# A two-layer graph kernel: the features of pair 2 moved ahead of pair 0's propagation, pair 1's exponentials transposed on TensorE, column sums of the weights in four column tiles

## The chip, the cores and the metric

The kernel runs on one core of a Trainium2 chip. The metric is device time in microseconds of one execution, without a profiler; it is given as the median of several runs. Engines are named as the profile names them: PE is TensorE (matmul), DVE is VectorE, ACT is ScalarE, POOL is GpSimd, SP is SyncE, which here only issues DMAs.

## The reference, cut to what matters

For each of 128 graphs with 128 nodes of 512 features, a graph attention layer and then a hypergraph convolution, each with a residual and a layer norm:

```python
# layer 0, for each graph b and each of 8 heads h (64 features each)
feats = einsum('bnf,hfu->bhnu', X, W)
dense = leaky_relu(e_self[..., :, None] + e_neigh[..., None, :], 0.2)   # e_* = feats . a_self, a_neigh
att = softmax(dense - 1e10 * (1 - A), axis=-1)
x = layernorm(X + relu(einsum('bhij,bhju->bhiu', att, feats) + b))
# layer 1: P(v) = D^-1 H B^-1 H^T v with H = (adj != 0)
h = layer_norm(relu(P(x @ W1.T) + b1), gamma, beta)
x = layernorm(x + P(h @ W2.T) + b2)
```

Everything is float32. W is 512 x 512 over all heads, W1 is 1024 x 512, W2 is 512 x 1024.

## The kernel before, in words

**Pairs and stages.** The graphs are worked on in 64 pairs, p = 0 to 63. A pair passes through these stages. Its rows are loaded as `xb` (four DMAs of 128 KB in a blocked form, L129) and transposed on DVE to `xT` (L385, two per pair). The matrix product `pf` gives the features `ft` with the two scores of each head beside them. The scores of the neighbours go through DRAM (`rd`, L552) and come back broadcast to all partitions as `nb` (two DMAs of 512 KB, L570). POOL adds the mask (`masked`, L589), ACT the node's own score with the leaky slope (L605), DVE takes the row maximum `nm` (L611), and ACT exponentiates in place (L619), so that `nb` then holds the exponentials. These are transposed to `eT`. For pairs from 1 on this is done through DRAM: written in one piece per graph as `ed` (L623), read back in blocks as `eb` (L631), and transposed block by block on DVE (L640). For pair 0 PE transposes them (`e_transpose_first`, `pet`, L651) and copies bring them out of PSUM (L652). `pav` (L703) multiplies `eT` by `ft`; `attended` (L714, L734 and L735), `residual` (L751 to L760) and `rstds` (`vea`, L765) lead to the normalized `y` (ACT, L794).

**Layer 1.** `edges` (L421 to L428) makes H^T and its degrees from the adjacency `ab` (L137), `scale_edges` (`hB`, L435) scales them, and `propagator` and `r_evict` (`pd`, `R`, L451) give P as a matrix. `pz` multiplies y by `R`; `zT` is copied out (L829). The chain `ph` multiplies by W1, `h_sum` and `relu` (L866, L881) give `h`, and the chain `py` multiplies by W2. `skip` (L805) makes `o` from `y` and b2, to which the output is added later.

**Products in seven parts.** `pf`, `ph` and `py` are each done by `chain` as seven products of halves in place of eight, in the order 1, 2, 6, 5, 7, 4, 3, into three PSUM banks X, Y and W; between them ACT copies X out (L344). They need sums of quarter blocks: of the rows (`xS`, `zS`, `hS`, made by POOL) and of the weights (made once at the start; `second_sums`, L226, for W2, by `prepare_output_block_sums`; L249 for W1). Product 4 of `py` uses the last of W2's sums, which is called `t4` below. `columns` (L97) issues each matmul as two tiles of 64 columns.

**Weights at the start.** gamma, beta and the mean over h are folded into W2. For this `prepare_output` multiplies W2 by the two columns `gbs` (`pv`, L276), `prepare_output_spread` spreads the result over all partitions (`gw`, `bw`, L288), and `prepare_output_blocks` rewrites the blocks of W2 (L300). Pairs 0 and 1 use plain products for `pf` and transposes of x and adjacency on PE.

**Order.** Each engine works through its instructions in the order in which the program issues them. That order is written by hand: every step has a pair lag and a time, `at(lag, time, fn, ...)`; its place is (p + lag) * 38.6 + time, the dictionary `first` puts other values in place of it for the first pairs, and the list `todo` is sorted by it. So the numbers only sort and aren't real times. SP's queue holds all loads and stores in that order; an issue that waits for a buffer holds back everything behind it. `nb`, `xb`, `ab` and `hB` have one buffer each, `R` has three. PSUM has eight banks, which go round. When `pair 1's propagation` is spoken of, that is the `pz` at 87.06 us in the profile.

Of the kernel before, what the change touches and what calls it, by code (L numbers as in the profile page):

```python
# [8 lines left out]
F32 = mybir.dt.float32  # L9
# [11 lines left out]
def kernel(  # L21
# [45 lines left out]
    nc = tc.nc  # L67
# [180 lines left out]
        )[i]  # L248
        engine.tensor_tensor(dst, in0, in1, op=op)  # L249

    gbs = const.tile([P, KH, 2], F32, name="gbs")
    made = {}

    def prepare_vectors():
# [9 lines left out]

    def prepare_rows():

        made["sel"] = work.tile([2, 2, P], F32, tag="zT", name="sel")
        nc.gpsimd.tensor_copy(
            made["sel"], ident[:2, :2].unsqueeze(2).to_broadcast([2, 2, P])
        )  # L270

    def prepare_output():
        pv = made["pv"] = [bank(f"pv{j}") for j in range(2)]
        for blk, i, j in w2_blocks:
            for k in range(KH // 2):
                nc.tensor.matmul(  # L276
                    pv[j][:2, :QU], gbs[:, i * KH // 2 + k, :], blk[:, k, :],
                    start=(i == 0 and k == 0), stop=(i == 1 and k == KH // 2 - 1),
                )

    def prepare_output_sums():
        made["sums"] = const.tile([2, F], F32, name="sums")
        for j in range(2):
            nc.vector.tensor_copy(made["sums"][:, j * QU:(j + 1) * QU], made["pv"][j][:2, :QU])

    def prepare_output_spread(c, name):
        made[name] = bank(name)
# [38 lines left out]
    def chain(kind, lag, times, multiply, w, extra=0, since=0, until=PAIRS):  # L326

        tag = "chain" if w == HALF else "half"

        def product(p, s, i):
            where, start = {1: ("X", 1), 2: ("Y", 1), 6: ("X", 0), 5: ("W", 1), 7: ("X", 0),
                            4: ("X", 0), 3: ("W", 0)}[i]
            if start:
                s[kind, where] = bank(f"{kind}{where}_{p}")
            multiply(s, i, s[kind, where], start)

        def copy(p, s, i):
            n = w + (extra if i < 2 else 0)
            t = s[kind, i] = work.tile([P, HALF if w == HALF else FW], F32, tag=f"{tag}_{i}", name=f"{kind}{i}_{p}")
            nc.scalar.copy(t[:, :n], s[kind, "X"][:, :n])  # L344

        for i, t in zip((1, 2, 6, 5, 7, 4, 3), times):
# [190 lines left out]
    @step(1, 25.0)  # L537
    def spread_rows(p, s):


        rows = work.tile([P, B], F32, tag="rows", name=f"rows_{p}")
        nc.vector.transpose(
            rows.rearrange("p (c x) -> p c x", c=2),
            s["ft"][:, :, :, :2].rearrange("p g h c -> p c (g h)"),
        )
        shape = [B, NB, B] if p == 0 else [NB, B, B]
        rd = s["rd"] = dram.tile(shape, F32, tag="rd", name=f"rd_{p}")
        if p == 0:
            for b in range(NB):
                (nc.sync, nc.scalar)[b % 2].dma_start(rd[:, b, :], rows[b * B:(b + 1) * B])  # L550
        else:
            nc.sync.dma_start(rd.rearrange("b c j -> (b c) j"), rows)  # L552

    def blocked(p, t):

        dims = "p (h b j) -> p b h j" if p == 0 else "p (b h j) -> p b h j"
        return t.rearrange(dims, b=NB, h=H)

    @step(1, 27.0)
    def neighbours(p, s):  # L560
        s["nb"] = work.tile([P, 2, H * N], F32, tag="nb", name=f"nb_{p}")
        for g in range(2):
            dst, src, hs = s["nb"][:, g, :], s["rd"], slice((2 + g) * H, (3 + g) * H)
            if p == 0:
# [5 lines left out]
            queue.dma_start(dst, src.partition_broadcast(P))  # L570
# [74 lines left out]
    def e_transpose_first(p, s, g, q):  # L645
        if (g, q) == (0, 0):
            s["eT"] = work.tile([P, 2, H, N], F32, tag="eT", name=f"eT_{p}")
        t = bank(f"pet_{g}{q}")
        for h in range(HH):
            n = (q * HH + h) * N  # L650
            nc.tensor.transpose(t[:, h * N:(h + 1) * N], s["nb"][:, g, n:n + N], ident)  # L651
# [470 lines left out]
    for t, fn, *args in (  # L1122
# [24 lines left out]
        (120.7, prepare_hidden, (nc.gpsimd, 2)), (110.6, prepare_hidden, (nc.vector, 3)),  # L1147
        (15.5, prepare_output_vectors, ()), (16.0, prepare_output, ()),
        (78.3, prepare_rows, ()), (78.79, prepare_output_sums, ()),
        (78.99, prepare_output_spread, (0, "gw")), (98.0, prepare_output_spread, (1, "bw")),  # L1150
        (98.1, prepare_output_bias, ()), (98.2, prepare_output_blocks, (slice(0, 1),)),
        (99.75, prepare_output_blocks, (slice(1, 2),)),
        (117.8, prepare_output_blocks, (slice(2, 3),)),
        (118.1, prepare_output_blocks, (slice(3, 4),)),
# [36 lines left out]
    for p, time, fn, *args in (  # L1191
# [5 lines left out]
        (1, 15.6, plain_features_out), (1, 97.9, adj_transpose_first),  # L1197
        (0, 78.8, e_transpose_first, 0, 0), (0, 78.85, e_transpose_first, 0, 1),
        (0, 78.9, e_transpose_first, 1, 0), (0, 78.93, e_transpose_first, 1, 1),
    ):  # L1200
        todo.append((time, run, (fn, p, args)))
    for p in range(PAIRS):
        if p > 1:
            todo.append(({2: 79.5, 3: 143.1}.get(p, p * T), load, (p,)))
            todo.append((16.2 if p == 2 else p * T + (19.0 if p == 3 else 2.0), load_blocks, (p,)))
            todo.append((p * T + (28.5 if p == 2 else 20.5), load_edges, (p,)))
        for lag, time, name, pairs, fn, args in steps:
            if p not in pairs:
                continue
# [66 lines left out]
```

## Time and profile before

| what | value |
|---|---|
| median of 3 runs | 2395.96 us |
| lowest and highest | 2395.58, 2396.99 us |
| the profiled execution, own time | 2395.3 us |
| its span, first to last instruction | 2393.4 us |
| granted TensorE clock, mean | 0.996 of full |
| busy: PE, DVE, ACT, POOL | 2360.8, 2089.6, 1528.5, 1825.6 us |
| PE busy in 0 to 45, 45 to 90, 90 to 135 us | 34.28, 40.26, 41.00 us |
| DVE busy in the same | 29.89, 44.17, 39.28 us |

Busy time is the sum over an engine's instructions; idle time of PE is 2393.4 less 2360.8, about 33 us, most of it in the first 160 us. The profile prints a line of kernel code as L and its number. In a timeline a line is the start in us, the duration in us, the engine, the line, the operation, its result and inputs with their shapes, and the number of instructions taken together; in brackets stands the idle time of the engine just before and the instruction that ended it.

### The profile page before, as it was taken

Reading aid. Unit: us, or ns where it says so; the run is one execution under the profiler, and the core shown is the slowest. Engines: PE = TensorE matmul, PEld = TensorE weight load, DVE = VectorE, ACT = ScalarE, POOL = GpSimd, SP = SyncE. Lnnn points to the kernel's source line nnn. Section 1 sums busy time; section 2 is a strip of 40 time slices with the busy share of each in tenths; the row PEclk is TensorE's granted clock in tenths of the full one; section 3 lists DMA queues with packets and bytes.
Section 4 is the critical chain, followed back from the end, with each engine's and each line's share of the span. In section 5 each row is a group of like instructions: output and inputs, shape, how many; then the busy total and the mean of one; then the engine's idle time right before and its main releaser. Section 6 shows DMA issues by size and latency. Waiting matters only on the chain.

```text
span 2393.4 us, 80729 instructions
## 1 busy us (share of the span) xinstructions
PE 2360.8 (99%) x32309; PEld 2026.8 (85%) x32309; DVE 2089.6 (87%) x4456; ACT 1528.5 (64%) x4481; POOL 1825.6 (76%) x2060
## 2 busy tenths in 40 slices
PE   7899999999999999999999999999999999999998
PEld 6788887888888888888888888888888888888886
DVE  7989888898898898898898888988988988988975
ACT  4565765756667667667667666666676676676662
POOL 5877786777877877877877778778778778778774
PEclk9999999999999999999999999999999999999999
DMA  6555454555554555555545555544545555555541
GB/s 197 133 148 150 143 144 134 159 143 147 151 148 144 149 148 148 151 143 154 144 142 157 141 147 155 146 146 147 150 143 153 147 150 139 148 156 140 149 128 37
DMA packets 431134, 347.09 MB, mean 145 GB/s; under 512 B 151440, under 2 KB 380328, under 8 KB 430760
## 3 DMA queue, kind: packets, MB, share of 16 engines
q1 hardware_dynamic: 427288, 337.46, 49.5%
q8 instruction: 256, 4.19, 0.7%
q10 hardware_dynamic: 3472, 4.47, 0.6%
q14 instruction: 118, 0.97, 0.2%
HBM read 239.08 MB, written 102.73 MB: 143 GB/s over the span
## 4 chain that ended last, share of the span: by engine, by line
PE 89%; DMA 4%; DVE 3%; ACT 1%; POOL 1%; issue 1%; SPq 1%; DVEq 0%; POOLq 0%; ACTq 0%
PE phX L97 17%; PE pyX L97 17%; PE pfX L97 8%; PE pyW L97 8%; PE phW L97 8%; PE pav L703 5%; PE phY L97 4%; PE pz L97 4%; PE pfW L97 4%; PE pq L97 4%; PE pyY L97 4%; PE pfY L97 2%; DMA ed<-nb 1%; PE pd L97 1%; DMA nb<-rd 1%
## 5 line engine op out<-in xcount | busy, mean ns | idle before, releaser
L344 ACT COPY py<-pyX 128x257 f32<-128x257 f32 x189 | 70.7, 374 | 538.5 <-PE pyX L97 465.6
L97 PEld LDWEIGHTS phX<-zS,w_sb 128*64 128x64 f32 x6144 | 350.6, 137 | 36.3 <-POOL ft L742 23.1
L97 PE MATMUL phX<-zS,w_sb 128*64 128x128 f32 x6144 | 373.4, 273 | 2.6 <-ACT ph L344 2.6
L904 POOL TENSOR_TENSOR sq<-sq 128x512 f32<-128x512 f32 (+2 forms) x384 | 343.9, 896 | 20.1
L589 POOL TENSOR_TENSOR nb<-nb,neg 128x512 f32<-128x512 f32 x256 | 319.9, 1284 | 23.1 <-DMA nb<-rd 12.7
L605 ACT ACTIVATE nb<-nb,ft 128x128 f32<-128x128 f32 x1020 | 325.1, 392 | 13.7 <-POOL nb L589 13.7
L619 ACT ACTIVATE nb<-nb,nm 128x128 f32<-128x128 f32 x1024 | 319.4, 392 | 4.2 <-DVE nm L611 4.0
L767 POOL TENSOR_TENSOR rso<-veo,mhalf 128x2 f32<-128x2 f32 x63 | 44.2, 701 | 338.4 <-DVE veo L765 338.4
L97 PE MATMUL pyX<-w_sb,hS 128*64 128x257 f32 x2016 | 245.1, 380 | 0.0
L97 PE MATMUL pyX<-w_sb,h 128*64 128x257 f32 x2016 | 243.7, 379 | 0.5 <-ACT py L344 0.5
L97 PE MATMUL pyW<-w_sb,hS 128*64 128x256 f32 x2016 | 243.3, 378 | 0.0
L881 ACT ACTIVATE h<-h,vecs 128x128 f32<-128x128 f32 x768 | 239.4, 394 | 2.0 <-DVE h L866 1.4
L611 DVE TENSOR_REDUCE nm<-nb 128x4 f32<-128x512 f32 x256 | 175.2, 684 | 48.8 <-ACT nb L605 46.2
L97 PEld LDWEIGHTS pyX<-w_sb,h 128*64 128x64 f32 x2016 | 173.7, 136 | 46.2 <-ACT py L344 0.9
L97 PEld LDWEIGHTS pyW<-w_sb,hS 128*64 128x64 f32 x2016 | 174.7, 136 | 43.6 <-issue 0.3
L742 POOL TENSOR_TENSOR ft<-ft,b_bc 128x512 f32<-128x512 f32 x128 | 203.9, 1613 | 6.1 <-ACT ft L533 6.1
L97 PEld LDWEIGHTS pyX<-w_sb,hS 128*64 128x64 f32 x2016 | 168.7, 137 | 38.7 <-issue 0.8
L640 DVE STREAM_TRANSPOSE eT<-eb 128x512 f32<-128x512 f32 x252 | 163.5, 685 | 5.7 <-DMA eb<-ed 4.7
L805 DVE SCALAR_TENSOR_TENSOR o<-y,b_bc 128x512 f32<-128x512 f32 x128 | 164.7, 1325 | 0.0
L1006 DVE SCALAR_TENSOR_TENSOR y<-y,rsh,bw_bc 128x512 f32<-128x512 f32 x126 | 150.1, 1229 | 14.9 <-POOL rsh L1002 14.9
L469 POOL TENSOR_TENSOR hS<-h 128x512 f32<-128x512 f32 x126 | 162.1, 1287 | 0.0
L892 ACT ACTIVATE sq<-h 128x512 f32<-128x512 f32 x256 | 160.6, 629 | 2.1
(178 smaller groups left out, 5672.4 us busy)
## 6 DMA issues: line engine op xcount, KB each, us to landing
nb<-rd SPq DMA_DIRECT2D x127, 512.0 KB, 5.6
ed<-nb SPq DMA_DIRECT2D x126, 512.0 KB, 3.4
eb<-ed SPq DMA_DIRECT2D x504, 128.0 KB, 2.9
x<-in_x_dram SPq DMA_DIRECT2D x64, 512.0 KB, 4.0
out_dram<-o SPq DMA_DIRECT2D x63, 512.0 KB, 2.9
xb<-in_x_dram SPq DMA_DIRECT2D x248, 128.0 KB, 5.5
a<-in_adj_dram SPq DMA_DIRECT2D x64, 128.0 KB, 2.4
w<-in_adj_dram SPq DMA_DIRECT2D x128, 64.0 KB, 5.0
```

Of the source, the lines that this page charges most:

```text
L97: nc.tensor.matmul(to[rows], lhs[:, rows], rhs, start=start, stop=stop, skip_group_check=True)
L469: engine.tensor_tensor(t[:, i], in0, in1, op=op)
L589: nc.gpsimd.tensor_tensor(t, t, neg[:, :, None, :].to_broadcast([P, NB, HH, B]), op=ALU.add)
L605: nc.scalar.activation(t, t, AF.Prelu, bias=s["ft"][:, g, h, 0:1], alpha=SLOPE)
L611: nc.vector.tensor_reduce(s["nm"][:, g, hs], scores(p, s, g, hs).rearrange("p b h j -> p h b j"), AX.XY, ALU.max, negate=True,)
L619: nc.scalar.activation(t, t, AF.Exp, bias=s["nm"][:, g, h:h + 1])
L640: nc.vector.transpose(s["eT"][:, g, hs, :].rearrange("p h (b i) -> p h b i", b=NB), s["eb", g][:, :, hs, :].rearrange("p b h j -> p h b j"),)
L742: nc.gpsimd.tensor_tensor(t, t, b0_bc.rearrange("p (h u) -> p h u", h=H), op=ALU.add)
L805: nc.vector.scalar_tensor_tensor(s["o"][:, g, :], s["y"][:, g, :], 2.0, b2_bc, op0=ALU.mult, op1=ALU.add)
L881: nc.scalar.activation(dst[:, k, :], src[:, k, :], AF.Relu, bias=b1_sb[:, c:c + 1])
L892: nc.scalar.activation(s["sq"][:, g, q * KH // 2:(q + 1) * KH // 2, :], hid(s, g, q), AF.Square, scale=DH ** -0.5,)
L904: nc.gpsimd.tensor_tensor(t[:, :n, :], t[:, :n, :], t[:, n:2 * n, :], op=ALU.add)
```

## The change

Three things are done, all in the first pairs.

- **Column sums.** `gbs` is padded from 2 to 32 columns, and the 32 matmuls of `pv` become 16, of which four at a time write to four column tiles of 32 in one bank; `sel` sums the four tiles while it spreads them, and the sums are copied in one piece.
- **Pair 2's features.** Pair 2's `xb` is loaded ahead of the W1 blocks. Its `xT` transposes, `xS` sums and five of its `pf` products (1, 2, 6, 5, 7) now stand before pair 0's `pz`, the other two (4, 3) right behind it.
- **Pair 1's exponentials** are transposed on PE, as those of pair 0, with all four copies out of PSUM on DVE; `ed` and `eb` begin with pair 2. `rd` of pair 1 is written in pair 0's layout, with four DMAs for one.

To fit these, the times of other steps move. On DVE, `edges(1)`, the rewriting of W2's blocks, the fourth sum of W1 and pair 0's `skip` (now two separate steps) change places; `t4`, `edges(2)` and `hB(2)` move from before pair 1's `attended` to behind its `residual`, where `edges(2)`, `hB(2)`, `R(1)`, `vea(1)` and then `t4` follow one another. On SP, the `xb` loads of pair 3 stand behind the `nb` loads of pair 2 (before: ahead of them). From pair 1's propagation on, the order on every engine is unchanged.

The core of the diff:

```diff
-    gbs = const.tile([P, KH, 2], F32, name="gbs")
+    gbs = work.tile([P, KH, B], F32, tag="y", name="gbs")
+    nc.gpsimd.memset(gbs, 0.0)
+    one = small.tile([P, 2], F32, tag="one", name="one", bufs=1)
...
     def prepare_output():
-        pv = made["pv"] = [bank(f"pv{j}") for j in range(2)]
-        for blk, i, j in w2_blocks:
-            for k in range(KH // 2):
-                nc.tensor.matmul(
-                    pv[j][:2, :QU], gbs[:, i * KH // 2 + k, :], blk[:, k, :],
-                    start=(i == 0 and k == 0), stop=(i == 1 and k == KH // 2 - 1),
-                )
+
+        t = made["pv"] = bank("pv")
+        for n in range(2):
+            for j in range(2):
+                for c in range(NB):
+                    k = 2 * c + n
+                    blk = w2_blocks[2 * (k // (KH // 2)) + j][0]
+                    nc.tensor.matmul(
+                        t[c * B:(c + 1) * B, j * QU:(j + 1) * QU], gbs[:, k, :],
+                        blk[:, k % (KH // 2), :], start=(n == 0 and j == 0), stop=(n == 1),
+                        skip_group_check=True,
+                    )
...
-        shape = [B, NB, B] if p == 0 else [NB, B, B]
+        shape = [B, NB, B] if p < 2 else [NB, B, B]
...
-        (nc.scalar.copy if q else nc.vector.tensor_copy)(
+        (nc.scalar.copy if q and p == 0 else nc.vector.tensor_copy)(
...
-        at(2, tt, e_transpose, g, q, since=1)
+        at(2, tt, e_transpose, g, q, since=2)
...
-        at(2, (6.2, 10.9)[g], e_write, g, since=1)
-        at(2, (10.0, 14.9)[g], e_read, g, since=1)
+        at(2, (6.2, 10.9)[g], e_write, g, since=2)
+        at(2, (10.0, 14.9)[g], e_read, g, since=2)
...
-        (126.57, prepare_output_block_sums, (nc.vector, slice(2, 3))),
-        (141.0, prepare_output_block_sums, (nc.vector, slice(3, 4))),
+        (132.6, prepare_output_block_sums, (nc.vector, slice(2, 3))),
+        (144.2, prepare_output_block_sums, (nc.vector, slice(3, 4))),
...
-        ("edges", 0): 14.46, ("edges", 2): 119.2,
-        ("x_transpose", 2, 0): 120.5, ("x_transpose", 2, 1): 121.1, ("scale_edges", 0): 14.47, ("propagator", 0): 14.55,
+        ("edges", 0): 14.46, ("edges", 2): 144.05, ("scale_edges", 2): 144.06,
+        ("x_transpose", 2, 0): 75.4, ("x_transpose", 2, 1): 78.7,
...
+        ("pf_product", 2, 1): 78.991, ("pf_copy", 2, 0): 78.9915, ("pf_product", 2, 2): 78.992,
+        ("pf_product", 2, 6): 78.993, ("pf_copy", 2, 1): 78.9935, ("pf_product", 2, 5): 78.994,
+        ("pf_product", 2, 7): 78.997, ("f_sum", 2, 0, 0, 0, "Y"): 97.85, ("pf_copy", 2, 2): 110.35,
+        ("f_sum", 2, 1, 1, 2, "W"): 110.36, ("pf_product", 2, 4): 116.71,
+        ("pf_product", 2, 3): 116.72, ("f_sum", 2, 0, 1, 1, "W"): 116.8,
+        ("spread_rows", 2): 117.86, ("f_sum", 2, 1, 0, None, "X"): 117.85, ("neighbours", 2): 131.2,
+        ("skip", 0, 0): 126.58, ("skip", 0, 1): 132.5, ("py_product", 0, 2): 140.5, ("scale_edges", 0): 14.47, ("propagator", 0): 14.55,
...
+        (1, 124.95, e_transpose_first, 0, 0), (1, 124.96, e_transpose_first, 0, 1),
+        (1, 130.41, e_transpose_first, 1, 0), (1, 130.42, e_transpose_first, 1, 1),
...
-            todo.append(({2: 79.5, 3: 143.1}.get(p, p * T), load, (p,)))
-            todo.append((16.2 if p == 2 else p * T + (19.0 if p == 3 else 2.0), load_blocks, (p,)))
-            todo.append((p * T + (28.5 if p == 2 else 20.5), load_edges, (p,)))
+            todo.append(({2: 80.35, 3: 143.1}.get(p, p * T), load, (p,)))
+            todo.append((14.02 if p == 2 else p * T + (19.0 if p == 3 else 2.0), load_blocks, (p,)))
+            todo.append(({2: 105.7, 3: 146.85}.get(p, p * T + 20.5), load_edges, (p,)))
```

More of the change, by code (lines that the diff above doesn't have):

```diff
@@ L265, in prepare_rows @@
     def prepare_rows():
-        made["sel"] = work.tile([2, 2, P], F32, tag="zT", name="sel")
-        nc.gpsimd.tensor_copy(
-            made["sel"], ident[:2, :2].unsqueeze(2).to_broadcast([2, 2, P])
-        )
+        nc.vector.tensor_reduce(
+            one, ident.rearrange("p (c r) -> p r c", c=NB)[:, :2], AX.X, ALU.add
+        )
+        made["sel"] = work.tile([P, 2, P], F32, tag="so", name="sel")
+        nc.gpsimd.tensor_copy(made["sel"], one.unsqueeze(2).to_broadcast([P, 2, P]))
     def prepare_output():
-        pv = made["pv"] = [bank(f"pv{j}") for j in range(2)]
-        for blk, i, j in w2_blocks:
-            for k in range(KH // 2):
-                nc.tensor.matmul(
-                    pv[j][:2, :QU], gbs[:, i * KH // 2 + k, :], blk[:, k, :],
-                    start=(i == 0 and k == 0), stop=(i == 1 and k == KH // 2 - 1),
-                )
+        t = made["pv"] = bank("pv")
[9 more added lines that the diff above has]
+                    )
     def prepare_output_sums():
-        made["sums"] = const.tile([2, F], F32, name="sums")
-        for j in range(2):
-            nc.vector.tensor_copy(made["sums"][:, j * QU:(j + 1) * QU], made["pv"][j][:2, :QU])
+        made["sums"] = work.tile([P, F], F32, tag="sq", name="sums")
+        nc.vector.tensor_copy(made["sums"], made["pv"])
     def prepare_output_spread(c, name):
@@ L344, in copy @@
             nc.scalar.copy(t[:, :n], s[kind, "X"][:, :n])
+        product.__name__, copy.__name__ = f"{kind}_product", f"{kind}_copy"
         for i, t in zip((1, 2, 6, 5, 7, 4, 3), times):
@@ L545, in spread_rows @@
         )
-        shape = [B, NB, B] if p == 0 else [NB, B, B]
+        shape = [B, NB, B] if p < 2 else [NB, B, B]
         rd = s["rd"] = dram.tile(shape, F32, tag="rd", name=f"rd_{p}")
-        if p == 0:
+        if p < 2:
             for b in range(NB):
-                (nc.sync, nc.scalar)[b % 2].dma_start(rd[:, b, :], rows[b * B:(b + 1) * B])
+                (nc.sync, nc.scalar)[b % 2 if p == 0 else 0].dma_start(rd[:, b, :], rows[b * B:(b + 1) * B])
         else:
@@ L554, in blocked @@
     def blocked(p, t):
-        dims = "p (h b j) -> p b h j" if p == 0 else "p (b h j) -> p b h j"
+        dims = "p (h b j) -> p b h j" if p < 2 else "p (b h j) -> p b h j"
         return t.rearrange(dims, b=NB, h=H)
@@ L563, in neighbours @@
             dst, src, hs = s["nb"][:, g, :], s["rd"], slice((2 + g) * H, (3 + g) * H)
-            if p == 0:
+            if p < 2:
                 src = src[hs].rearrange("h b j -> (h b j)")
@@ L647, in e_transpose_first @@
             s["eT"] = work.tile([P, 2, H, N], F32, tag="eT", name=f"eT_{p}")
-        t = bank(f"pet_{g}{q}")
+        t = bank(f"pet_{p}_{g}{q}")
         for h in range(HH):
-            n = (q * HH + h) * N
-            nc.tensor.transpose(t[:, h * N:(h + 1) * N], s["nb"][:, g, n:n + N], ident)
-        (nc.scalar.copy if q else nc.vector.tensor_copy)(
+            nc.tensor.transpose(
+                t[:, h * N:(h + 1) * N],
+                s["nb"][:, g, (q * HH + h) * N:(q * HH + h + 1) * N], ident,
+            )
+        (nc.scalar.copy if q and p == 0 else nc.vector.tensor_copy)(
             s["eT"][:, g, q * HH:(q + 1) * HH, :].rearrange("p h n -> p (h n)"), t
@@ L1146 @@
         (79.0, prepare_hidden, (nc.gpsimd, 0)), (79.1, prepare_hidden, (nc.gpsimd, 1)),
-        (120.7, prepare_hidden, (nc.gpsimd, 2)), (110.6, prepare_hidden, (nc.vector, 3)),
+        (120.7, prepare_hidden, (nc.gpsimd, 2)), (123.15, prepare_hidden, (nc.vector, 3)),
         (15.5, prepare_output_vectors, ()), (16.0, prepare_output, ()),
         (78.3, prepare_rows, ()), (78.79, prepare_output_sums, ()),
[L1150 to L1154, printed above, removed]
+        (78.995, prepare_output_spread, (0, "gw")), (123.2, prepare_output_spread, (1, "bw")),
+        (123.7, prepare_output_bias, ()), (112.0, prepare_output_blocks, (slice(0, 1),)),
+        (117.8, prepare_output_blocks, (slice(1, 2),)),
+        (119.0, prepare_output_blocks, (slice(2, 3),)),
+        (121.75, prepare_output_blocks, (slice(3, 4),)),
         (126.5, prepare_output_block_sums, (nc.gpsimd, slice(0, 2))),
-        (126.57, prepare_output_block_sums, (nc.vector, slice(2, 3))),
-        (141.0, prepare_output_block_sums, (nc.vector, slice(3, 4))),
+        (132.6, prepare_output_block_sums, (nc.vector, slice(2, 3))),
+        (144.2, prepare_output_block_sums, (nc.vector, slice(3, 4))),
         (100.0, prepare_mean_columns, ()),
@@ L1163 @@
         ("nodes", 0): 12.9, ("write_nodes", 0): 12.92, ("spread_nodes", 0): 15.9,
-        ("edges", 0): 14.46, ("edges", 2): 119.2,
-        ("x_transpose", 2, 0): 120.5, ("x_transpose", 2, 1): 121.1, ("scale_edges", 0): 14.47, ("propagator", 0): 14.55,
+        ("edges", 0): 14.46, ("edges", 2): 144.05, ("scale_edges", 2): 144.06,
+        ("x_transpose", 2, 0): 75.4, ("x_transpose", 2, 1): 78.7,
+        ("x_sums", 2, 0): 78.71, ("x_sums", 2, 1): 78.72, ("x_sums", 2, 2): 78.73,
+        ("x_sums", 2, 3): 78.74,
+        ("pf_product", 2, 1): 78.991, ("pf_copy", 2, 0): 78.9915, ("pf_product", 2, 2): 78.992,
[5 more added lines that the diff above has]
+        ("skip", 0, 0): 126.58, ("skip", 0, 1): 132.5, ("py_product", 0, 2): 140.5, ("scale_edges", 0): 14.47, ("propagator", 0): 14.55,
         ("r_evict", 0): 97.845,
         ("spread_rows", 1): 15.72, ("nodes", 1): 15.55, ("write_nodes", 1): 15.85,
-        ("edges", 1): 110.4, ("scale_edges", 1): 110.5, ("neighbours", 1): 80.1,
-        ("propagator", 1): 121.7, ("spread_nodes", 1): 80.3, ("r_evict", 1): 121.8,
+        ("edges", 1): 97.95, ("scale_edges", 1): 97.96, ("neighbours", 1): 80.1,
+        ("propagator", 1): 130.3, ("spread_nodes", 1): 80.3, ("r_evict", 1): 144.1,
         ("leaky", 0, 1, 1): 77.65, ("leaky", 0, 0, 1): 73.6, ("largest", 0, 0, 1): 75.3,
@@ L1184 @@
         ("r_evict", 2): 160.4,
-        ("nodes", 3): 154.6, ("write_nodes", 3): 154.7, ("skip", 0): 132.5,
+        ("nodes", 3): 154.6, ("write_nodes", 3): 154.7,
     }
@@ L1196 @@
         (1, 14.5, plain_features, 0), (1, 14.6, plain_features, 1),
-        (1, 15.6, plain_features_out), (1, 97.9, adj_transpose_first),
+        (1, 15.6, plain_features_out), (1, 78.996, adj_transpose_first),
         (0, 78.8, e_transpose_first, 0, 0), (0, 78.85, e_transpose_first, 0, 1),
         (0, 78.9, e_transpose_first, 1, 0), (0, 78.93, e_transpose_first, 1, 1),
+        (1, 124.95, e_transpose_first, 0, 0), (1, 124.96, e_transpose_first, 0, 1),
+        (1, 130.41, e_transpose_first, 1, 0), (1, 130.42, e_transpose_first, 1, 1),
     ):
@@ L1220 @@
                 time = {
-                    ("product", 2): 24.22 if (lag, time) > (3, 20.0) else time,
-                    ("product", 5): 29.5 if (lag, time) > (3, 20.0) else time,
+                    ("py_product", 2): 24.22, ("py_product", 5): 29.5,
                     ("squares", 0): 26.5, ("squares", 1): 26.6, ("h_sums", 2): 22.3,
```

## Prediction, made before the changed kernel had been run

> **What bounds the kernel now.** I read the windows first (columns: stretch, its length, busy us and instructions of PE, PE's weight loads, VectorE, ScalarE and GpSimd, then granted clock, DMA share, GB/s).
>
> ```profile
> 45.00:90.00 45.00, 40.26 (x536) 34.43 (x536) 44.17 (x84) 28.44 (x84) 39.59 (x37) 0.93 0.47 119
> 1000.00:1038.00 38.00, 38.00 (x522) 33.17 (x520) 34.22 (x72) 24.20 (x71) 29.98 (x34) 1.00 0.48 148
> ```
>
> In the middle of the run PE is busy for 38.00 of 38 us: TensorE bounds the steady part. The change reorders only the first 87 us or so; from pair 1's propagation (`pz` at 87.06 here) on, each engine's order is as it was. So the prizes are PE's idle time and slow clock at the start. PE's timeline names them (start, duration, operation, count, idle before and its releaser):
>
> ```profile
> 33.17 3.62 PE L276 MATMUL pv<-w_sb,gbs 128*2 128x256 f32 x16
> 36.73 1.97 PE L651 MATMUL pet<-ident,nb 128*128 128x128 f32 x16
> ...
> 47.23 3.68 PE L97 MATMUL pz<-R,y 128*64 128x128 f32 x32 [4.05 <-ACT y L794]
> 50.69 2.24 PE L97 MATMUL phX<-zT,w_sb 128*64 128x128 f32 x32
> ...
> 87.06 1.94 PE L97 MATMUL pz<-R,y 128*64 128x128 f32 x32
> ...
> 96.00 1.97 PE L97 MATMUL phX<-zS,w_sb 128*64 128x128 f32 x32 [1.92 <-ACT ph L344]
> ...
> 116.62 1.97 PE L703 MATMUL pav<-ft,eT 128*64 128x65 f32 x60 [1.72 <-DVE eT L640]
> ```
>
> The hole of 4.05 us before pair 0's `pz` is what the change fills. It costs clock too, as a second set of windows shows:
>
> ```profile
> 43.00:47.20 4.20, 0.18 (x1) 0.00 (x0) 4.06 (x11) 2.00 (x6) 1.96 (x3) 0.68 0.73 222
> 47.20:50.70 3.50, 3.47 (x33) 3.48 (x35) 3.40 (x13) 2.43 (x6) 2.93 (x6) 0.50 0.36 67
> ```
>
> At half clock these 32 matmuls take 3.68 us, against 1.94 at 87.06; with 0.3 us of the following `phX` some 2.0 us are lost. The holes from there to 160 us (0.69, 0.68, 0.48, 0.92, 1.92, 1.72, 0.62) sum to 7.0.
>
> But between 45 and 90 VectorE is busy for 44.17 of 45 us: that stage is VectorE's, and the chain of waits runs there almost wholly on DVE. Its rows ahead of pair 1's propagation, then three DMA issues of SyncE:
>
> ```profile
> 67.92 4.81 DVE L805 SCALAR_TENSOR_TENSOR o<-y,b_bc 128x512 f32<-128x512 f32 x2
> ...
> 75.39 2.15 DVE L226 TENSOR_TENSOR w_sb<-w_sb 128x1024 f32<-128x1024 f32 x1
> 77.46 1.13 DVE L385 STREAM_TRANSPOSE xT<-xb 128x512 f32<-128x512 f32 x1
> ...
> 84.34 0.17 DVE L765 TENSOR_SCALAR vea<-mva 128x2 f32<-128x2 f32 x1
> ```
>
> ```profile
> 69.30 1.86 SPq L129 DMA_DIRECT2D xb<-in_x_dram  x4
> ...
> 78.54 0.94 SPq L570 DMA_DIRECT2D nb<-rd  x2
> ...
> 80.40 1.78 SPq L112 DMA_DIRECT2D w<-in_adj_dram  x2
> ```
>
> `xb` of pair 3 is issued at 69.30, ahead of `nb` of pair 2, and has landed when DVE transposes it at 77.46.
>
> **What the Trainium skill says.** "TensorE: Matmul & The Clock Gate", Part 1: The HAM clock gate, has the clock halved after an idle window of about 3.4 us and restored after about 3.4 us of work; the trace agrees (4.05 us idle, then 0.50 until 51.35, 4.1 us after work resumed). "TensorEngine Tiling (Array Packing)", Key Properties: column tiles work independently, and a change of tiling drains the engine; the trace agrees for two tiles (32 half-width matmuls in 1.75 us start to start) and doesn't show four. "SBUF — State Buffer" calls the port pair that VectorE and GpSimd share "an exclusive lock"; the trace fits (one `skip`, L805, takes from 0.68 to 2.87 us). "DMA: Bandwidth & Descriptors", Queues, rings and completion order: each DMA engine takes descriptors in ring order; the trace fits (the second `nb` landed at 86.05, `w` behind it, issued at 80.40, at 87.11).
>
> **The change, part by part.**
>
> *Column sums in four tiles.* 32 matmuls, 29.72 to 36.73, become 16: 1.75 us if the tiles run side by side, 3.5 if not. Worth nothing either way: the next PE work, the transposes of pair 0's exponentials, waits for ScalarE's last exponential at 37.64. Even twice the time would end by 36.7. The copy of the sums as one 128x512 in place of two of 256 costs DVE about 0.1.
>
> *Pair 2's features ahead of pair 0's `pz`.* Five of seven products (0.89 us each start to start, 4.45) move, with pair 1's `pt` (0.44), into 42 to 47.2; two follow `pz`. What goes with them: four `xb` loads (0.45 us of SP each) ahead of the W1 loads, two DVE transposes (2.1 us) between pair 0's row maxima, four sums on GpSimd after pair 0's masks (GpSimd was busy 0.53 of 3 us at 40 to 43). DVE has waits there for exponentials and loads, so I count nothing; if `xb` lands late behind `nb` of pair 0, up to +1; a gain is excluded, since `pz(0)` waits for the exponentials' chain. `vea(0)` stays at 45.0, `pz(0)` at 47.2, the hole falls to about 0.5, the clock stays up: 2.0 us and 4.45 us of work are off PE's later path. The next limit is then DVE, not PE.
>
> *Pair 1's exponentials on TensorE.* Off go two 512 KB writes (`ed`), eight 128 KB reads (`eb`), 4.2 us of SP's issues (0.35 + 1.74 + 0.34 + 1.73) and four DVE transposes (2.5). On come 16 PE transposes (1.75 to 1.97, as `pet` at 36.73) and four DVE copies out of PSUM (0.69 each, as L652 in the groups; 2.8): DVE +0.3. The last group ends, by PE's sum, at 47.2 + `pz` 1.75 + `pf` 2 × 0.89 + `ph` 7 × 1.75 + `bw` 0.9 + `pd` 0.44 + 1.75 = **66.1**; waits inside could only make it later.
>
> *The wait that this adds on SP.* There is one `nb` buffer. Pair 2's `nb` now waits for that last PE transpose, so its two issues fall at 66.4 to 67.3. Pair 3's four `xb` loads stand **behind** it: issued 67.3 to 69.2, with 1 MB ahead in the same rings. `nb` landed 7.08 us after its second issue at 78.97, 5.53 after that at 120.46: here 72.3 to 74. `xb`'s half megabyte at the 200 to 240 GB/s of these windows takes 2.2 to 2.6 more: **75.5** (74 to 77).
>
> *VectorE.* From 45.07 to 77.46 it did 32.4 us. Off that path go `t4` (w2's last block sum, L226, 2.1), `edges(2)` (2.4), `hB(2)` (1.8), pair 2's `xT` (2.0); on comes 0.3. So it reaches pair 3's `xT` at 69.5 (72 if the lock costs more), and stands some 5.5 us. Queued behind that wait: pair 1's attended features, both residuals, `edges(2)`, `hB(2)`, `R(1)`, `vea(1)`, and only then `t4`. Before, `xT` to `vea` took 6.88; with `edges(2)` 2.0 and `hB(2)` 0.7 (0.48 at 50.03, 1.90 at 64.28) it is 9.7: **`vea(1)` at 85.2** (83.5 to 86.7), against 84.34: +0.9.
>
> *PE behind that.* `py`'s products 1, 2, 6, 7, 5 with `pav(1)` between run out at about 66.1 + 5 × 1.75 + 1.87 + 1.1 (wait for `hS`) = 77.8. Product 4 needs `t4`, which ends 1.3 to 2.1 after `vea(1)`: 86.9. PE idles 9 us, the clock halves for 4.1 us once more (2.05 lost, 1.7 to 3.4 by where the clock's window falls): products 4, 3 and `pz(1)`, 3 × 1.75, end at **94.2 against 88.81, +5.4**.
>
> *What of it survives.* ScalarE has the copies of `py` and `zT(1)` between pair 2's leaky steps, so these slip too: first exponential of pair 2 at 96.6 for 94.11, `ph`'s copy behind it at 97.9 for 95.29, so `phX` resumes at 98.5 for 96.00 (+2.5; the hole of 1.92 takes up most of the rest). PE is then busy up to `pav(2)`, where 1.72 us of slack leave +0.8 by its own work. Through DVE the way there is `vea` +0.9, `t4` +1.3 to 2.1, less up to 1.0 of contention that the shift may spare (w's sums at 86.14 to 89.4 took 3.2 us, 0.7 at 94.91), then `dr`, DRAM and `eT`: +1.2 to +3.0. The later of the two decides: +2.0 at 116.62, and nothing behind takes it up but part of the 0.62 at 153.8.
>
> The profiled execution was 2395.3 us (span 2393.4 and 1.9 around it), 0.7 below the median of the three runs, 2396.0. The +2.0 is made on its span; put on the median, which is to be forecast, it gives **2398.0**. Some 0.2% (4.8 us) is what a measurement of this kernel can tell from no change.
>
> **Rivals.** (a) *`xb` isn't late*: DVE doesn't wait at `xT`. For it: without `ed` and `eb` the rings are less loaded (share 0.47 before), and DVE may come there at 72; against it: the 1 MB ahead. `vea(1)` comes at 69.5 to 72 + 9.7 = 79.2 to 81.7, `t4` by 83, PE idles 4 to 5 us and `pz(1)` ends at 86 to 88; DVE's way is -5 to -2.6 plus `t4` 1.3 to 2.1, less 1.0 of contention: -1 to -5, 2391 to 2395. (b) *Slower*: the same queue on SP, with `xb` after 77.5 because PE's transposes end later than their bare sum or the rings carry `rd` and `ab` as well. Then `vea(1)` is at 87.5 or later, `t4` takes 2.15 under GpSimd's lock, `pz(1)` ends at 97.5; the slack at `pav(2)` is used up, so each us comes out: +5 to +8, 2401 to 2404. It decides from about 2.5 us later than my 75.5. (c) *The four tiles don't run side by side*, or draining between tilings costs a few tenths per change: hidden before the exponentials, and 0.5 us on PE around the transposes of pair 1, which isn't the bound there: 2398 to 2398.5.
>
> **How the numbers follow.** Forecast with (c) 0.55 (2396 to 2401, 0.03 of it over 2400.8), (a) 0.20 (0.08 of it below 2391.2), (b) 0.25 (0.01 of it under 2400.8). Faster 0.08, within 0.2% 0.65, slower 0.27. A range of 2392.5 to 2403 leaves out half of (a) and a third of (b).
>
> **What would show it.** Right: `pz(0)` still near 47.2, at 1.9 us, with `pf` ahead of it; `nb` of pair 2 issued near 67; DVE idle some 5 us before L385, released by DMA `xb`; PE idle some 9 us before a `pyX`, released by DVE L226, and slow clock behind it; `pav(2)` and all after it some 2 us later. Wrong: no idle time at L385; `pz(0)` moved by over 1 us; or a shift at `pav(2)` that isn't there at the end.

## The result: 1% slower, and the profile after

The changed kernel takes 2420.33 us (median of 4, 2419.69 to 2422.37); the kernel before took 2395.77 beside it. The ratio is 1.0104 (95% interval 1.0086 to 1.0121): 24.6 us slower, where +2.0 was forecast and the range ended at 2403. The profiled execution has a span of 2419.1 us against 2393.4, so 25.7 us have to be found.

TensorE's timeline of the changed kernel, in the lines that answer to those shown of before:

```profile
33.44 2.33 PE L658 MATMUL pet<-ident,nb 128*128 128x128 f32 x8 [2.33 <-POOL nb L597]
...
39.44 1.31 PE L658 MATMUL pet<-ident,nb 128*128 128x128 f32 x4 [3.68 <-issue]
...
43.18 3.71 PE L687 MATMUL pav<-ft,eT 128*64 128x65 f32 x64 [0.33 <-DVE eT L662]
...
53.78 1.97 PE L97 MATMUL pz<-R,y 128*64 128x128 f32 x32 [1.01 <-ACT y L804]
...
97.57 3.68 PE L97 MATMUL pyX<-w_sb,h 128*64 128x256 f32 x16 [10.60 <-DVE w_sb L226]
...
102.92 1.93 PE L97 MATMUL pz<-R,y 128*64 128x128 f32 x32
...
128.60 1.97 PE L713 MATMUL pav<-ft,eT 128*64 128x65 f32 x60 [0.44 <-DVE eT L648]
```

The hole before pair 0's `pz` has shrunk from 4.05 to 1.01 us and `pz` runs at full clock, as the change intends. But `pz` itself starts at 53.78 in place of 47.23, the hole of 10.60 us before product 4 of `py` is new, and `pav(2)` is 12.0 us late (128.60 for 116.62). VectorE's timeline has the two causes, each in brackets behind an `xT`:

```profile
37.26 1.08 DVE L393 STREAM_TRANSPOSE xT<-xb 128x512 f32<-128x512 f32 x1 [4.65 <-DMA xb<-in_x_dram]
...
45.90 1.90 DVE L761 SCALAR_TENSOR_TENSOR y<-y,x 128x512 f32<-128x512 f32 x1
...
51.55 0.17 DVE L775 TENSOR_SCALAR vea<-mva 128x2 f32<-128x2 f32 x1
...
88.04 1.08 DVE L393 STREAM_TRANSPOSE xT<-xb 128x512 f32<-128x512 f32 x1 [10.06 <-DMA xb<-in_x_dram]
...
96.14 0.16 DVE L775 TENSOR_SCALAR vea<-mva 128x2 f32<-128x2 f32 x1
96.21 1.22 DVE L226 TENSOR_TENSOR w_sb<-w_sb 128x1024 f32<-128x1024 f32 x1
```

`vea(0)` is 6.6 us later than before, `vea(1)` 11.8 (84.34 before). A smaller cause stands between the two brackets: the residual (L761) of 1.90 us. The kernel before had there:

```profile
40.58 0.69 DVE L751 SCALAR_TENSOR_TENSOR y<-y,x 128x512 f32<-128x512 f32 x1
...
44.99 0.17 DVE L765 TENSOR_SCALAR vea<-mva 128x2 f32<-128x2 f32 x1
```

SyncE's issues for the two waits:

```profile
23.76 2.15 SPq L129 DMA_DIRECT2D xb<-in_x_dram  x4
...
75.43 0.94 SPq L578 DMA_DIRECT2D nb<-rd  x2
76.42 4.35 SPq L129 DMA_DIRECT2D xb<-in_x_dram  x4
```

The first `xb` is issued at 23.76 to 25.9 and lands at 37.06. The second stands behind `nb`, as forecast; its four issues take 4.35 us in place of 1.86, and it lands at 88.0.

The windows (columns as in the prediction) show the rest of the loss:

```profile
36.50:46.70 10.20, 6.18 (x73) 4.97 (x74) 8.44 (x15) 3.62 (x10) 4.98 (x6) 0.50 0.49 165
...
91.10:101.40 10.30, 3.83 (x18) 2.44 (x20) 9.92 (x28) 3.38 (x10) 5.02 (x4) 0.50 0.10 16
```

```profile
1000.00:1038.00 38.00, 37.84 (x531) 32.89 (x529) 33.82 (x70) 24.26 (x71) 29.46 (x35) 1.00 0.50 143
```

In both of the first two windows TensorE's granted clock is 0.50, called half clock below, in the first of them while it had 6.18 us of work. And far behind the reordered part PE is no longer busy without a break. The shift against before is 12.1 us at `pz` of pair 3 (178.1 for 166.0) and 27.2 at pair 60 (2272.4 for 2245.2): **half of the loss arises where the two kernels issue the same instructions in the same order** (semaphore instructions left out, they do so on every engine from 99.17 us of the changed kernel on).

### The profile page after: what moved, and what is told of

It is laid out like the page before. It is cut to its first block, busy times and chain, and to the rows that moved or that the text cites. A ratio compares the mean times of both kernels' runs of the same rounds, so it can differ in the third digit from the quotient of the medians.

```text
span 2419.1 us, 80755 instructions
## 1 busy us (share of the span) xinstructions
PE 2362.9 (98%) x32325; PEld 2000.9 (83%) x32325; DVE 2081.0 (86%) x4456; ACT 1528.6 (63%) x4481; POOL 1824.1 (75%) x2061
## 4 chain that ended last, share of the span: by engine, by line
PE 70%; DMA 14%; DVE 5%; POOL 4%; ACT 3%; SPq 2%; issue 1%; DVEq 0%; POOLq 0%
PE pyX L97 14%; PE phX L97 13%; PE pyW L97 7%; PE phW L97 6%; PE pfX L97 6%; DMA ed<-nb 6%; PE pav L713 4%; PE pz L97 4%; PE phY L97 3%; PE pyY L97 3%; DMA nb<-rd 3%; PE pq L97 3%; PE pfW L97 3%; DMA eb<-ed 2%; DMA rd<-rows 2%; ACT nb L613 2%
## 5 line engine op out<-in xcount | busy, mean ns | idle before, releaser
L597 POOL TENSOR_TENSOR nb<-nb,neg 128x512 f32<-128x512 f32 x256 | 319.5, 1282 | 48.4 <-DMA nb<-rd 36.5
```

The costliest lines, as they stand in the source:

```text
L597: nc.gpsimd.tensor_tensor(t, t, neg[:, :, None, :].to_broadcast([P, NB, HH, B]), op=ALU.add)
```

## A late mode: the theory for the second half

From the timelines of TensorE and SyncE I took, for each pair, the time from one `pz` to the next, and when in it the next pair's `nb` is issued. There are two kinds of pairs, and I call a stretch of late ones the late mode. On-time ones have `nb` at 26.6 us behind `pz` and take 36.37 us. Late ones have it at up to 30 and take up to 38.5 (once, in before, 40.4). Counting as late what is over 27.5 (pairs 3 to 59), before has 12 late pairs, all but two of them up to pair 14, and the periods behind them have a mean of 36.89; the changed kernel has 31, all but three up to pair 30, with a mean of 37.05. 31 x 0.68 less 12 x 0.52 is 14.9 us: about what the shift grows by (15.1 from pair 3 to pair 60; some 1.5 come back in the last pairs). SyncE's issues of an on-time pair (before), then of a late one (changed):

```profile
827.21 1.88 SPq L129 DMA_DIRECT2D xb<-in_x_dram  x4
833.47 0.34 SPq L623 DMA_DIRECT2D ed<-nb  x1
836.40 1.82 SPq L631 DMA_DIRECT2D eb<-ed  x4
```

```profile
849.23 1.86 SPq L129 DMA_DIRECT2D xb<-in_x_dram  x4
852.28 0.34 SPq L631 DMA_DIRECT2D ed<-nb  x1
858.63 1.74 SPq L639 DMA_DIRECT2D eb<-ed  x4
```

On time, `xb` has 6.3 us from its first issue to `ed`, and `eb` follows 2.9 us behind `ed`. Late, `ed` comes 3.1 us behind `xb`, whose 512 KB are still on the way (the last 128 KB landed at 856.1), and `eb` follows after 6.4 us. (Means over the pairs of the changed kernel: 5.3 us late, 3.5 on time.) What comes of it is in VectorE's timeline at the end of that pair:

```profile
869.87 1.30 DVE L648 STREAM_TRANSPOSE eT<-eb 128x512 f32<-128x512 f32 x2 [1.36 <-DMA eb<-ed]
...
871.59 0.24 DVE L550 STREAM_TRANSPOSE rows<-ft 128x32 f32<-128x32 f32 x1
```

The next pair's `rows` stand behind `eT`, `rd` behind `rows`, `nb` behind `rd`, the exponentials behind `nb`, and `ed` behind those. As I read it, the loop closes on itself, and when it lags it is as long as TensorE's own period or longer, so TensorE keeps waiting and the loop doesn't catch up. The experiments test what makes it long (e3, e4) and what ends it (f1).

## The experiments

All ratios are to the kernel before on the same chip, where it ran at medians of 2399 to 2400 us.

**e1: pair 2's transposes behind the last row maximum.**

```diff
-        ("x_transpose", 2, 0): 75.4, ("x_transpose", 2, 1): 78.7,
+        ("x_transpose", 2, 0): 78.67, ("x_transpose", 2, 1): 78.7,
```

> The changed kernel, with the two transposes of pair 2's xb put behind pair 0's last row maximum on VectorE instead of between the row maxima; all else as changed. Theory (a wait at the head of VectorE's queue): the changed kernel lost 6.6 us at vea of pair 0 (51.55 for 44.99) because xb of pair 2 landed at 37.06 and the remaining row maxima, and so the exponentials, stood behind its transpose, which waited 4.65 us. Here the last maximum ends near 36, the transposes start at 37 and vea of pair 0 falls to 47 to 48.5; pz of pair 0 near 50; vea of pair 1 about 4 us earlier than 96.1; whole run 4 us faster, or up to 15 if the slow pairs up to 1250 us get fewer. Rival (TensorE bound by the five products now ahead of pz, or by half clock): vea of pair 0 stays above 50.

`vea(0)` came at 48.87 (51.55; expected 47 to 48.5), `vea(1)` at 93.43 (96.14). So 2.7 of the 6.6 us were exponentials queued behind a transpose that waited. What remains is the two transposes themselves (2.1 us, now on the path), 1.2 us at the residual (L761, again 1.90 us), and a part of the half clock: the 16 `pet` took 4.82 us (1.97 before), which VectorE's transposes cover, and `pav` 3.73 (2.09). The total didn't follow: 1.0097 (1.0081 to 1.0113). The start's gain went into the late mode: 2.6 us at `pz` of pair 3 were gone at pair 60, behind 27 late pairs with a mean of 37.18. The expectation that the whole run is 4 us faster failed.

**e2: pair 3's `xb` ahead of pair 2's `nb`.**

```diff
-p * T + (19.0 if p == 3 else 2.0)
+({3: 131.1}.get(p, p * T + 2.0))
```

> The changed kernel, with pair 3's four xb loads issued by SyncE ahead of pair 2's two nb loads; all else as changed. Theory (SyncE's queue): VectorE's wait of 10.06 us at pair 3's transpose is the wait of nb for the last TensorE transpose plus 1 MB ahead in the rings; without it VectorE doesn't wait there, vea of pair 1 falls from 96.1 to 86 to 88 and TensorE's idle time of 10.6 us before product 4 of py to under 3; the run is 8 to 10 us faster, more if the slow pairs get fewer. Rival (VectorE would be late anyway through contention or the products of ph): vea of pair 1 above 92.

VectorE doesn't wait any more:

```profile
77.57 1.15 DVE L393 STREAM_TRANSPOSE xT<-xb 128x512 f32<-128x512 f32 x1
```

`vea(1)` came at 87.92, the hole before product 4 was 3.04 us. The mechanism held; of the 8.2 us gained at `vea(1)` the profile still has 7.8 at pair 60, and the total some 7 (1.0073, 1.0049 to 1.0097; runs from 2411 to 2423). The late mode is as it was, though, with 30 late pairs: `pz` of pair 3 is only 4.1 us later than before, that of pair 60 19.5.

**e3 and e4: `xb` behind `eb` from pair 4 on,** in the changed kernel and in the one before.

```diff
-p * T + (19.0 if p == 3 else 2.0)
+p * T + (19.0 if p == 3 else 15.0)
```

> The changed kernel, with the xb loads of every pair from 4 on issued behind the eb reads of the pair two before it, instead of ahead of that pair's ed writes. Theory (a late mode that keeps itself up): in the changed kernel some pairs up to 1250 us take 36.9 to 38.4 us instead of 36.37, because xb's 512 KB is issued some 1 us ahead of ed and delays its landing, which delays eb, eT, the rows of the next pair and its nb, and with these the next xb. With xb out of the way ed lands in about 3 us and the pairs take 36.4 from pair 6 on: some 10 to 14 us faster, 2406 to 2411. Rival (the lag comes from the start and lasts by other means, such as GpSimd or ScalarE): within 3 us of the changed kernel. Second rival: xb now comes too late for its transposes, every pair waits, over 2425.

> The kernel before with the same move of the xb loads from pair 4 on. Theory of the late mode: before loses only some 5 us in it (pairs 5 to 10), so 2391 to 2393. Rival without such a mode: 2396 as it was. Rival that xb comes too late: over 2400.

e3: 2406.0 us, 1.0028 (1.0020 to 1.0035), against 1.0104 of the changed kernel, with the start as bad as ever (`vea(1)` 95.20). Late pairs are still there (27), but cost less: their mean is 36.61, and `eb` follows `ed` after 3.92 us. e4: 2390.13 us, 0.9961 (0.9947 to 0.9976). The late mode is in the kernel before too (here 14 late pairs, with a mean of 36.75). That is not the whole gain, though: the two profiles differ by 2.6 us in all, nearly all of it before pair 3, and the ratio says 9; where the rest lies no trace shows.

The pair of them is the cleanest test of the second half. With the move in both kernels the change costs 16 us by the ratios (13 against g4, the repetition of e4 below) in place of 25, and the shift no longer grows: e3 is behind e4 by 12.9 us at `pz` of pair 3 and by 13.3 at pair 60.

**f1: more work for TensorE, once.**

```diff
-        for t, g, h in to:
+        for t, g, h in to * (4 if p == 4 else 1):
```

> The changed kernel with TensorE work added: pair 4's products of exponentials and features (pav) are computed four times over in place of once, 3 x 1.87 = 5.6 us more on TensorE, same results. Theory of the late mode: the loop nb, exponentials, ed, eb, eT, rows, nb lags behind TensorE by some 2 to 3 us and is as long as TensorE's own period, so it never catches up; if TensorE once stands back by 5.6 us the loop is ahead again, nb of later pairs is issued 26.6 us after pz (not 28 to 29.6), the pairs from 6 on take 36.37 us, and of the 14 us that the slow pairs cost some 10 or more don't arise: 2408 to 2414, faster in spite of added work. Rival (the slow pairs have another cause): 2426, the added work on top.

The total, 1.0121 (1.0096 to 1.0145; runs from 2422 to 2436), missed the expectation and lies where the rival had it, the added work on top. The profile, of one of the two faster runs (2423.53), shows more. From the very pair with the added work on, `nb` is at 26.6 and the pairs take 36.37 us, up to pair 23. Windows over 730 us, first the changed kernel, then f1:

```profile
220.00:950.00 730.00, 719.92 (x9932) 606.60 (x9928) 633.12 (x1355) 467.43 (x1375) 558.00 (x629) 1.00 0.52 145
```

```profile
220.00:950.00 730.00, 730.00 (x10134) 631.23 (x10132) 648.45 (x1384) 478.61 (x1407) 568.66 (x642) 1.00 0.53 147
...
1300.00:2000.00 700.00, 693.15 (x9559) 586.61 (x9556) 612.23 (x1308) 450.98 (x1329) 536.56 (x606) 1.00 0.52 146
```

PE is busy for all 730 us, and `vea` of pair 24 is 10.7 us earlier than in the changed kernel (941.72 for 952.37), in spite of 5.6 us more work. Then, at pairs 24 and 25, f1 fell back into the late mode and stayed to the end, where the changed kernel had left it at pair 31. So in this execution the loop was on time from the moment that TensorE stood back. It is one trace, and g2 below was on time over the same pairs without any such help, so chance isn't excluded; and what throws a kernel into or out of the mode at about pairs 24 to 31 is not shown.

**f2: all new waits undone** (e1, e2 and e3 together, and `t4` ahead of pair 3's transpose).

```diff
-        (144.2, prepare_output_block_sums, (nc.vector, slice(3, 4))),
+        (141.0, prepare_output_block_sums, (nc.vector, slice(3, 4))),
```

> The changed kernel with its new waits undone together: the transposes of pair 2 behind pair 0's last row maximum, pair 3's xb loads ahead of pair 2's nb, w2's last block sum ahead of pair 3's transpose, and xb behind the eb reads from pair 4 on. Theory (the waits and the late mode are all of the loss): start as fast as before or nearly, vea of pair 0 at 48.9, of pair 1 at 83 to 86, total 2388 to 2394, within 3 us of the kernel before with the same move of xb (2390.1): the moved features and TensorE transposes then buy about nothing, because VectorE bounds the start. Rival (the idea pays once its waits are gone): 2383 to 2386. Rival (something else of the change costs): over 2397.

0.9991 (0.9983 to 0.9999), `vea(0)` 48.28, `vea(1)` 85.64: some 9 us faster than e3 by the ratios, but hardly better than before, and slower than e4 and g4 (0.9961 and 0.9972). Against e4, which has `xb` in the same place, the change costs 16 us with its waits (e3) and 7 without. So the waits are the larger part and not all, as the second rival had it (over 2397; it was 2398.12): even without its waits the change doesn't pay.

**f3 and f4: without the features, and without pair 1's TensorE transposes,** both with `xb` behind `eb`.

In f3 pair 2's loads, `x_transpose`, `x_sums`, products and copies of `pf`, `f_sum`, `spread_rows` and `neighbours` have their times of before:

```diff
-14.02 if p == 2 else p * T + (19.0 if p == 3 else 2.0)
+16.2 if p == 2 else p * T + (19.0 if p == 3 else 15.0)
...
-        ("x_transpose", 2, 0): 75.4, ("x_transpose", 2, 1): 78.7,
+        ("x_transpose", 2, 0): 120.5, ("x_transpose", 2, 1): 121.1,
```

In f4 `rd` and `nb` of pair 1 have the layout of before, and `ed`, `eb` and the transposes on VectorE begin with pair 1:

```diff
-        at(2, tt, e_transpose, g, q, since=2)
+        at(2, tt, e_transpose, g, q, since=1)
...
-        (1, 124.95, e_transpose_first, 0, 0), (1, 124.96, e_transpose_first, 0, 1),
-        (1, 130.41, e_transpose_first, 1, 0), (1, 130.42, e_transpose_first, 1, 1),
```

> The changed kernel with pair 2's features put back where they were (loads, transposes, sums, products and their copies), TensorE transposes of pair 1 and column tiles kept, and xb behind the eb reads from pair 4 on. Pair 3's xb then stands ahead of pair 2's nb again. Theory (both lost waits come from moving pair 2's work forward: its xb at the head of VectorE's queue at 37, and its nb ahead of pair 3's xb): vea of pair 0 at 45, no wait at pair 3's transpose, 2389 to 2395 against 2390.1 of before with the same xb move and 2406 of the change with it. Rival (the TensorE transposes of pair 1, which hold nb, are the cause): over 2400.

> The changed kernel with pair 1's exponentials transposed through DRAM again (ed, eb, rd in one piece), all of the moved features and the column tiles kept, and xb behind the eb reads from pair 4 on. Theory: both waits stay, as xb of pair 2 still lands at 37 and pair 3's xb stands behind pair 2's nb, which now waits for ed instead of a TensorE transpose: vea of pair 0 near 51, of pair 1 at 94 or later, 2403 to 2410, like the change with the same xb move (2406). Rival (the TensorE transposes of pair 1 are what costs): 2390 to 2395.

f3: 0.9993 (0.9986 to 1.0000), `vea(0)` 46.55 (45 expected; `pet` took 4.82 us at half clock, the residual 0.69 again), `vea(1)` 88.02, no wait at L393. f4: 1.0020 (1.0012 to 1.0027), `vea(0)` 51.84, `vea(1)` 96.37 with 8.69 us of waiting at L393. So both waits belong to the moved features; pair 3's `xb` waits behind pair 2's `nb` whether that waits for TensorE or for `ed`. f3 stays slower than e4, its total above the expected 2395 (2397.8), so the rest of the change costs as well.

**g1, g3 and the control g4: one part alone,** on the kernel before with `xb` behind `eb`; g4 is e4 again.

Of the change g1 has only the padded `gbs` with `prepare_rows`, `prepare_output` and `prepare_output_sums`, and g3 only pair 1's `e_transpose_first`, the layout of `rd` and `nb` for it, and `ed` and `eb` from pair 2 on:

```diff
-    gbs = const.tile([P, KH, 2], F32, name="gbs")
+    gbs = work.tile([P, KH, B], F32, tag="y", name="gbs")
```

```diff
+        (1, 124.95, e_transpose_first, 0, 0), (1, 124.96, e_transpose_first, 0, 1),
+        (1, 130.41, e_transpose_first, 1, 0), (1, 130.42, e_transpose_first, 1, 1),
```

> The kernel before with xb behind the eb reads from pair 4 on, and of the change only the column sums in four column tiles (pv 1.9 us in place of 7.0). Theory (the short pv costs clock): TensorE then waits from 31 us for pair 0's exponentials, its clock halves near 35, pav of pair 0 takes 3.7 us in place of 2.1 and vea of pair 0 comes at 46.3 to 46.9 instead of 44.3 to 45.0; the run is 1 to 3 us slower than the control. Rival (what the prediction said: hidden): vea of pair 0 at 45.0 or earlier, no difference.

> The kernel before with xb behind the eb reads from pair 4 on, and of the change only pair 1's exponentials transposed on TensorE, in the place where the change has them; pair 3's xb ahead of pair 2's nb. Theory (VectorE bounds the stage and does the same amount): vea of pair 1 within 1.5 us of the control, total within 2 us of it. Rival (the transposes hold nb of pair 2, and 1.9 us of TensorE work, on the path): 3 us or more slower. Rival (the DMA way was the limit): 2 us or more faster.

> The control of this set: the kernel before with xb behind the eb reads from pair 4 on, once more. 0.996 of before.

g4: 0.9972 (0.9965 to 0.9979), `vea(0)` 44.72, `vea(1)` 83.96. In g1 the tiles do run side by side, but the short `pv` leaves TensorE idle and its clock halves, as its timeline has it:

```profile
33.88 4.82 PE L658 MATMUL pet<-ident,nb 128*128 128x128 f32 x16 [3.22 <-POOL nb L596]
38.63 3.74 PE L684 MATMUL pav<-ft,eT 128*64 128x65 f32 x64
```

`vea(0)` came at 45.78, 1.1 us later than in the control, less than expected; before, e4 and g4, which have the same start, lie between 44.29 and 44.99. The total is the control's: 0.9968 (0.9960 to 0.9976). g3: 0.9987 (0.9980 to 0.9994), 3.8 us over the control, as the first rival had it, with `vea(1)` at 87.38 (+3.4). Of that 1.2 us are there at `vea(0)` already (45.88); behind it VectorE waits 2.34 us for the `pf` products of pair 2, which stand behind the transposes on TensorE.

**g2: `pv` three times over, in f2.**

```diff
-        for n in range(2):
+        for n in (0, 1) * 3:
```

> The changed kernel with its new waits undone (as f2_waits_undone), and the four-tile column sums computed three times over, same results: TensorE stays busy until about 35. Theory (clock): pav of pair 0 takes 2.1 us again, vea of pair 0 falls from 48.3 to 46.3 to 47.0, and the run is 1 to 3 us faster than f2_waits_undone (ratio to before 0.9991) in spite of 3.9 us more work. Rival: vea of pair 0 stays at 48.3 or comes later.

0.9991 (0.9983 to 0.9998), `vea(0)` at 48.36: no gain. TensorE was busy until 35, but `pav` now stands behind VectorE's two transposes (a wait of 1.86 us), the clock fell at 40.8 all the same, and `pav` took 3.04 us (3.73 in f2). The residual began 0.6 us earlier than in f2 for it and lost that again: it took 2.60 us for 1.90. The expectation failed: in f2 the start hangs on VectorE first, and the clock is only the smaller part.

**The late mode, over all traces.** The table has the number of late pairs from 3 to 59, and the time from `pz` of pair 3 to that of pair 60 (57 pairs of 36.37 us would be 2073.1). Each run has one trace.

| traces | pair 1's transposes | `xb` | late pairs | `pz(3)` to `pz(60)`, us |
|---|---|---|---|---|
| changed, e1, e2 | TensorE | ahead of `ed` | 27 to 31 | 2094.3 to 2097.2 |
| e3, f2, f3, g3 | TensorE | behind `eb` | 26 to 29 | 2079.4 to 2081.3 |
| before | through DRAM | ahead of `ed` | 12 | 2079.2 |
| e4, f4, g1, g4 | through DRAM | behind `eb` | 11 to 16 | 2076.4 to 2082.6 |

How late the start is doesn't decide it. f4 starts as late as e3 (`vea(1)` at 96.37 and 95.20) and has 11 late pairs for 27; e2 and f2 start nearly on time (87.92 and 85.64) and have 30 and 29. What goes with a long late mode in these traces is pair 1's transposes on TensorE, and what makes it dear is `xb` ahead of `ed`. How a step of pair 1 reaches pair 30 isn't shown: the two go together in the traces, no more. f1 and g2, also with the transposes on TensorE, stand apart. But for a pair or two they are on time up to pair 23 and late from there to pair 59 (38 and 36 late pairs), g2 without any work added to pair 4 and with a `vea(1)` (85.76) like that of f2.

## Why the prediction was wrong, step by step

- **What bounds the kernel.** "TensorE bounds the steady part" was read from one window, at 1000 us. It is true of on-time pairs alone. Before itself has ten late pairs up to pair 14, and a hole of 2.32 us at 375.75, after which it came to be on time for the first time. I took that part for rigid. This is the step that failed for 14 of the 24.6 us: "nothing behind takes it up" is right, but the shift doesn't stay as it is, it grows from 12.1 to 27.2 us, because the loop through DRAM, with `xb` ahead of `ed`, keeps TensorE waiting pair after pair. With `xb` behind `eb` it stays (12.9 and 13.3 us, e3 against e4). What starts the long late mode is open; it goes with pair 1's transposes, not with the length of the delay.
- **Pair 2's features**: "DVE has waits there for exponentials and loads, so I count nothing; if `xb` lands late [...] up to +1". It was +6.6 at `vea(0)`: a wait of 4.65 us with two row maxima queued behind it, 2.1 us of transposes, the half clock, and 1.2 us at the residual. GpSimd, behind its four new sums of x, was then at a sum of W1 (44.90 to 47.25) that in before had ended ahead of the residual, at 40.5; without the moved features (f3) the residual took 0.69. The load lands 11.7 us behind its last issue, beside `nb` and the W1 blocks of ScalarE's queue (in 28 to 36.5 us the DMA engines are busy 0.99 of the time). I named the load and the queue, but didn't price the landing from the trace of before, where one of these loads, issued at 35.59, landed at 42.15.
- **Column sums**: "Worth nothing either way" holds for the total (g1), not for the start. The cover was real, but the work that I let shrink was what kept the clock up: 1.1 us at `vea(0)` in g1. The Trainium skill's "TensorE: Matmul & The Clock Gate", Part 1, has the clock fall after an idle window of about 3.4 us; I had used it for the hole that closes and not for the one that opens. The traces agree that idle time brings the clock down, but less of it was enough: in f3 PE stood idle for 1.62 us, was busy for 1.88 of the 3.41 us up to 36.59, and the clock fell there. The four tiles themselves behave as the Trainium skill's "TensorEngine Tiling (Array Packing)", Key Properties, says, side by side: 32 matmuls of some 0.39 us in 1.9 us, for 7.1 in before. (The trace has 32 matmuls in both kernels, where I wrote that they become 16: the program issues 16 in both, and each leaves two records.)
- **SP's wait**: the mechanism, its place and its order were right (e2). The size was off: 10.06 us for 5.5. `nb` could be issued at 75.4 and not 66.4, as the start was late by 6.6 and `ph` had waits of its own; and `xb` was there 12.6 us after that, where I had put 9.1, its own issues behind 1 MB taking 4.35 us in place of 1.86. The ring order that the Trainium skill's "DMA: Bandwidth & Descriptors", Queues, rings and completion order, states fits: the second `nb` landed at 83.98, `xb` behind it by 88.0. But its half megabyte took 4.1 us there where I had put 2.2 to 2.6, at a rate that only one of my windows shows (222 GB/s; the others have 67 to 148). Luck took some of it back: `xT` to `vea(1)` took 8.1 us, not 9.7.
- **PE behind that**: 10.60 us idle (9 forecast), clock at 0.50 behind it, product 4 at 3.68 us. The holes of 0.92, 1.92 and 1.72 us took up 3.9 us between `pz(1)` (+15.9) and `pav(2)` (+12.0), much as forecast (+5.4 to +0.8).
- **Pair 1's transposes**: "DVE +0.3" is the other mis-sized term. It counts VectorE's own work and no wait for TensorE, where the transposes push back pair 2's `pf`. g3 has +3.4 us at `vea(1)`, 2.34 of them that wait.
- **Rival (b)** named the right chain and direction, decided by `xb` after 77.5; it was 88.0. Its price of +5 to +8 lacked both the late start and the late mode. Of my signs of being wrong two came: `pz(0)` moved by 6.6 us, and the shift at `pav(2)`, 12.0, is not the one at the end, 25.7.

Of the versions built, the one that beats both kernels is the one before with `xb` behind `eb` (e4 and g4): 0.9961 and 0.9972 of before.

## What to carry to other kernels

Work moved ahead brings its loads with it: before a step goes to the head of an in-order queue, read when its data lands and list what then stands behind it, on the engine and on the DMA queue. Where a pipeline's loop through DRAM is about as long as its bound engine's period, it can lag for dozens of rounds and charge a little in each, and one window in the middle doesn't show it; so tabulate the period pair by pair before calling a stage bound, and keep loads that can wait (`xb`) out of the way of the loop's own (`ed`). Speeding up covered matmuls can cost clock for the ones behind them.

## What the runs showed that was not expected

In one execution 20 pairs behind 5.6 us of added TensorE work ran without a wait, where late ones had lost 0.68 us each. Four 128 KB loads took 1.86 us to issue on a free queue and 4.35 behind 1 MB (4.49 in f4). TensorE's clock stayed at half for 10.2 us: 2.34 us of work between 39.91 and 43.33 didn't bring it back, and 3.41 without a break, from there to 46.74, did.
